# Zero fill at the head of the program, mix weights after it, convolution folding in the linear attention's steps

## The chip, the core and the metric

The kernel runs on one core of a Trainium2 chip. The metric is the device time of one execution in microseconds (us); the median of a few executions is taken. One more execution was recorded by the hardware profiler, and all times inside the kernel come from that one. The engines are named as the profile names them: PE (matrix multiplications; PEld loads their weights), DVE (vector), ACT (scalar, activations), POOL (general purpose) and SP, which only issues transfers. ACT and POOL issue transfers too. An engine works through its own list of instructions in order; an ending "q" (SPq, ACTq) marks the part that waits and issues.

## What is computed

Two layers of a graph network act on 1250 nodes with 512 channels and 40000 edges. The first layer adds three branches to the input: an attention over the edges, a linear attention over all nodes, and a feed-forward part. The second layer adds a graph convolution, a global attention and a lookup among experts. Cut to what matters here:

```python
xn = layernorm(x)
# linear attention ("mix"): all nodes
k = relu(xn @ Wk + bk) + eps;  v = xn @ Wv + bv;  q = relu(xn @ Wq + bq) + eps
h = layernorm(q @ (k.T @ v) / den @ Wo + bo + xn)
mix = layernorm(relu(h @ W1 + b1) @ W2 + b2 + h)
# edge attention ("gnn"): softmax over the edges of each source node
s[e] = q[src[e]] . k[dst[e]] / 8 + att_bias[e]
# second layer: the convolution has no function between its two matrices
conv = (A @ xn @ W_gcn + b_gcn) @ W_dense + b_dense
```

Since nothing stands between `W_gcn` and `W_dense`, the kernel multiplies them once (`W_gcn @ W_dense`, kept as `wgd_d`) and once the bias (`b_gcn @ W_dense + b_dense + b_proj`, kept as `bsum_d`). A third small product, `fold_q`, is that of the second layer's query weights with the vector `w_q`. These three are "the convolution's folding" below; nothing reads them before the second layer.

## The kernel before, in words

The edge attention is done on a dense table: `adj` in device memory has one row of nine numbers for each of 1280 x 1280 (source, target) pairs, eight for the heads' summed exp(bias) and one for the count of edges, 59 MB in all. Three things make it.

* **The fill.** Lines 221 to 228 write zeros: POOL clears a small tile `zrow`, and SP issues four transfers of 14400 KB and a small one.
* **The edge steps.** `scatter_edges` (L303) is a generator: each `pump(1)` runs one step over six columns of 128 edges, and there are 53 steps, of two batches of three columns (105 batches). A step loads keys (`kr`, L311), DVE compares them (`eq` at L325, `eqx` at L335), PE adds the weights of equal keys (L317), and DVE leaves sums and row numbers (`tot` L342, `idx` L348).
* **The scatter.** POOL issues one indirect transfer for each column, 313 in all (L351), that adds 128 rows of `tot` to `adj`. The first needs the whole fill. `tot` and `idx` have 48 buffers.

When all edges are in, SP loads `adj` in ten slabs of 5760 KB (L652), and the edge attention begins.

Between fill and slabs lies the dense work, into which the edge steps are woven by `pump` calls:

* A: normalise `xn`, transpose it (L157, L168, L171). `x` comes by the ACT queue.
* B: keys and values of the linear attention, ten tiles of 128 nodes (L487 to L493): per tile four matmuls with Wk and four with Wv, then `kp` and `va` on DVE, which add rows of `mixrows`. Wk, Wv and mixrows come by the ACT queue (L454 to L456).
* C: `kv` (L502). D: queries `qpT` (L514).
* E: ten steps, one per tile (L524 to L545): attention, Wo, layer norm, `h`.
* F: its feed-forward part, ten tiles (L556 to L566).
* G, H: weights of the edge attention, `zT`, `kT` and `q_d` (L583 to L605). I: values `gva` (L606 to L610).
* J: the convolution's folding (L613 to L635), with its own loads of 1024 KB weights, its results stored by SP.

A second generator, `weight_products` (L400), computes other products of weights (`fs` on ACT, L419) in pieces; `next(products)` runs one piece in each of the steps of C, D and E until it is used up, which in the list of PE is in the third step of E.

A transfer's end is told by one of eight semaphores (DMAHW0 to 7) that SP's and ACT's transfers take in turn. A transfer that takes a semaphore waits until the last one with the same semaphore has ended. So a transfer of one queue can wait for one of the other; such waits stand in the built instruction list next to those on data.

Of the kernel before, what the change touches and what calls it, by code (L numbers as in the profile page):

```python
# [66 lines left out]
def tile_gps_layers(ctx: ExitStack, tc: tile.TileContext, a, out):  # L67
# [12 lines left out]

    def ps_tr(shape=(P, 512), name="tr"):
        return psum.tile(list(shape), F32, tag="tr", bufs=2, name=name)


    ident = const.tile([P, P], F32, name="ident")
# [107 lines left out]
        mm(ps, [(w[:, c, m * P:(m + 1) * P], xT[:, c, c0:c0 + cn]) for c in range(xT.shape[1])])  # L193


    adj = dram.tile([NROW, CH], F32, name="adj")
    key_d = dram.tile([EC, P], F32, name="key_d")
    cnt_d = dram.tile([NP, NP], F32, name="cnt_d")
    q_d = dram.tile([P, KC, NP], F32, name="q_d")
    xm_d = dram.tile([NP, C], F32, name="xm_d")  # L200
    xb_d = dram.tile([NP, C], F32, name="xb_d")
    att_d = dram.tile([P, KC, NP], F32, name="att_d")
    deg_d = dram.tile([P, NP], F32, name="deg_d")
    w1f_d = dram.tile([NEXP, P, KC, 256], F32, name="w1f_d")
    wgd_d = dram.tile([P, KC, C], F32, name="wgd_d")
    wqd_d = dram.tile([P, KC, NKEYS], F32, name="wqd_d")
    bsum_d = dram.tile([P, C], F32, name="bsum_d")

    s_xn = ctx.enter_context(ExitStack())
    pxn = s_xn.enter_context(tc.tile_pool(name="xn", bufs=1, side="right"))
    xn = pxn.tile([P, NT, C], F32, tag="xn", name="xn")

    s_edge = ctx.enter_context(ExitStack())
    pe = s_edge.enter_context(tc.tile_pool(name="edge", bufs=1, side="right"))
    s_tmp = ctx.enter_context(ExitStack())
    ptmp = s_tmp.enter_context(tc.tile_pool(name="edgetmp", bufs=1, side="right"))

    zrow = pe.tile([P, 1800], F32, name="zrow")
    nc.gpsimd.memset(zrow, 0.0)
    adj_p = adj[0:NKEY, :].rearrange("(p r) c -> p (r c)", p=P)
    step = 16 * 1800
    for z0 in range(0, NKEY * CH // P, step):
        nc.sync.dma_start(adj_p[:, z0:z0 + step].rearrange("p (a f) -> p a f", f=1800),
                            zrow[:, None, :].to_broadcast([P, 16, 1800]))
    nc.sync.dma_start(adj[NKEY:NROW, :].rearrange("(p r) c -> p (r c)", p=P), zrow[:, :(G + 1) * CH])

    def edge_column(name, src, width, dt, fill):  # L230
        t = ptmp.tile([P, EC, width] if width > 1 else [P, EC], dt, name=name)
# [71 lines left out]
    def scatter_edges():  # L303
# [3 lines left out]
        def load_keys(c0):  # L307
            cn = min(G + B, EC - c0)
            kr = pew.tile([P, (G + B) * P], F32, name="kr")
            queue = nc.scalar if c0 == 0 else nc.sync  # L310
            queue.dma_start(kr[:, :cn * P],  # L311
                            bass.AP(tensor=key_d.tensor, offset=key_d.offset + c0 * P, ap=[[0, P], [1, cn * P]]))
            return kr
# [24 lines left out]
                add_pairs(acc, eq, n, weights(c), fresh and c == 0)  # L338

        def scatter(acc, cnt, c0, g, place):  # L340
            tot = pew.tile([P, B, CH], F32, name="tot", bufs=48)
            nc.vector.tensor_reduce(tot[:, :g], acc[:, :g].rearrange("p c (t n) -> p c n t", t=3),  # L342
                                    axis=AX.X, op=OP.add)
            row = pew.tile([P, B], F32, name="row")
            nc.vector.scalar_tensor_tensor(row[:, :g], cnt[:, :g], 1.0, keyrel[:, c0:c0 + g],
                                           op0=OP.is_equal, op1=OP.mult)
            idx = pew.tile([P, B], I32, name="idx", bufs=48)
            nc.vector.tensor_tensor(idx[:, :g], row[:, :g], spare[:, place:place + g], op=OP.add)  # L348
            near, cur = (scattered[-1] if scattered else []), []
            for c in range(g):  # L350
                st = nc.gpsimd.indirect_dma_start(  # L351
                    out=adj, out_offset=bass.IndirectOffsetOnAxis(ap=idx[:, c:c + 1], axis=0),
                    in_=tot[:, c, :], in_offset=None, compute_op=OP.add)
                for x in cur + near:
                    tc.declare_no_dep(st.ins, x.ins, reason="rows of a batch and of the one next to it differ")
                for x in (scattered[-2] if len(scattered) > 1 else []):
                    tc.add_manual_dep(st.ins, x.ins.name, SYNC, reason="rows of batches may agree")
                cur.append(st)
            scattered.append(cur)
# [40 lines left out]
    def weight_products(pool):  # L400


        def turned(name):
            wT = pool.tile([P, KC, C], F32, tag="fwT", name=name + "T")
            for k in range(KC):
                if k % 2 == 0:
                    w = pool.tile([P, KC, 256], F32, tag="fw", name="fw", bufs=2)
                    nc.sync.dma_start(w, a[name].rearrange("(c p) o -> p c o", p=P)[:, :, k * P:(k + 2) * P])
                ps = ps_tr((P, KC, P))
                for c in range(KC):  # L410
                    nc.tensor.transpose(ps[:, c, :], w[:, c, k % 2 * P:(k % 2 + 1) * P], ident)
                nc.scalar.copy(wT[:, k, :].rearrange("p (c q) -> p c q", c=KC), ps)
            return wT

        def product(wT, w, m, to):
            ps = ps_mm((P, 256))
# [25 lines left out]
                    yield  # L442

    with (tc.tile_pool(name="mix", bufs=1) as pm, tc.tile_pool(name="mixw", bufs=2) as pw,
# [3 lines left out]
        for t in range(NT):  # L451
            n = TAIL if t == NT - 1 else P
            nc.scalar.dma_start(xn[:n, t, :], a["x"][t * P:t * P + n, :])
        wk = load_w(pm, "L0_mix_Wk", KC, C, bufs=2, eng=nc.scalar)  # L454
        wv = load_w(pm, "L0_mix_Wv", KC, C, bufs=2, eng=nc.scalar)
        rows = rows_bc(pm, a["mix_rows"], len(MIX_ROWS), name="mixrows", eng=nc.scalar)  # L456

        def row(name):
            return rows[:, MIX_ROWS.index(name), :]
# [122 lines left out]
    with tc.tile_pool(name="gqkv", bufs=2) as pq:  # L582
# [23 lines left out]
        for t in range(NT):  # L606
# [1 line left out]
            node_mm(ps, zT, t, wv)  # L608
            nc.vector.tensor_tensor(va[:, t, :], ps, gbv[:, 0, :], op=OP.add)
            pump(1)  # L610


        brow = rows_bc(pq, a["l1_rows"], len(L1_ROWS), name="l1rows")  # L613
        wg = load_w(pq, "gcn_WgT", KC, C, bufs=3)
        wd = load_w(pq, "L1_gnn_W_dense", KC, C, bufs=3)
        wqn = load_w(pq, "l1_Wq", KC, C, bufs=3)
        for m in range(KC):
            ps = ps_mm()
            mm(ps, [(wg[:, c, m * P:(m + 1) * P], wd[:, c, :]) for c in range(KC)])
            qs = pq.tile([P, 512], F32, tag="qs", name="qs", bufs=3)  # L620
            nc.scalar.copy(qs, ps)
            nc.sync.dma_start(wgd_d[:, m, :], qs)
            pump(1)
        ps = ps_mm()
        mm(ps, [(col("gcn_b", c).to_broadcast([P, P]), wd[:, c, :]) for c in range(KC)])
        qs = pq.tile([P, 512], F32, tag="qs", name="qs", bufs=3)
        nc.vector.tensor_tensor(qs, ps, brow[:, 0, :], op=OP.add)
        nc.vector.tensor_tensor(qs, qs, brow[:, 1, :], op=OP.add)
        nc.sync.dma_start(bsum_d, qs)
        bd = pq.tile([P, KC, H], F32, name="bd")  # L630
        nc.vector.tensor_tensor(bd, own_head, col("l1_wq", 0, 4)[:, :, None].to_broadcast([P, KC, H]), op=OP.mult)
        ps = ps_tr((P, KC, H))
        for m in range(KC):
            mm(ps[:, m, :], [(wqn[:, c, m * P:(m + 1) * P], bd[:, c, :]) for c in range(KC)])
        nc.scalar.copy(fold_q[:, :, :H], ps)  # L635
        pump(EC)
    s_edge.close()
    s_xn.close()
# [1353 lines left out]
```

## Time and profile before

| what | us |
|---|---|
| median of three executions | 2455.51 (2454.69 to 2459.25) |
| profiled execution | 2448.96 |
| its span, first to last instruction | 2447.2 |
| PE busy | 2001.3 (82%) |
| DVE busy | 1523.3 (62%) |
| POOL busy | 696.5 (28%) |
| first and last scatter issued | 175.32, 772.57 |
| last `gva` (end of I) begins | 776.64 |
| first slab issued | 797.86 |
| first scores of the edge attention | 816.07 |

The profiled execution's time is its span and 1.8 us around it, and lies 6.6 us below the median. In the rows of the profile the first two numbers are the start and the length in us, if nothing else is said. "xN" is a number of instructions. A fp32 matmul of the program counts twice in the trace. "[0.30 <-X]" is how long the engine was idle before the instruction, and what ended that. In a table by stretches, each engine has its busy time in the stretch; after them stand the TensorE clock that was granted (1.00 is full), the busy share of the transfer engines, and the GB/s that they moved.

### The profile page before, as it was taken

The page shows a single profiled execution, that of the slowest core. Times are in us where ns is not written, and L with a number is a line of the kernel's source. Part 1 is how long each engine was busy: PE and PEld are TensorE (multiplying, and loading weights), DVE is VectorE, ACT ScalarE, POOL GpSimd, SP SyncE. Part 2 cuts the span into 40 slices and gives each one's busy share as a digit, 9 for nine tenths or more (in the row PEclk, how much of TensorE's full clock was granted, in tenths as well). Part 3 has the DMA queues.
Part 4 walks back from the last instruction along what each step waited for, and adds up shares of the span by engine and source line. Part 5 has one row for each costly group of instructions (what it writes and reads, how often), then busy time and mean ns, then how long its engine had stood idle before and what let it go on. Part 6 is the DMA issues. An engine that isn't in the chain of part 4 may idle for free.

```text
span 2447.2 us, 29595 instructions
## 1 busy us (share of the span) xinstructions
PE 2001.3 (82%) x10548; PEld 1182.2 (48%) x10548; DVE 1523.3 (62%) x4868; ACT 789.3 (32%) x1483; POOL 696.5 (28%) x448
## 2 busy tenths in 40 slices
PE   0299697684499699999799988999999999978853
PEld 0146465442245366666445445567444545555521
DVE  3539858789891599999432444456222233499998
ACT  0101001010000467777331255556211123244553
POOL 2018888888885000000000000000000000045665
PEclk9999788775699799999899999999899999989975
DMA  9987554345643666554510100000410002000000
GB/s 393 422 349 188 101 116 64 42 87 108 153 89 77 248 233 226 193 222 145 177 64 22 49 1 1 1 1 1 153 35 26 26 9 69 22 22 9 10 9 16
DMA packets 132591, 255.78 MB, mean 105 GB/s; under 512 B 51677, under 2 KB 87190, under 8 KB 130780
## 3 DMA queue, kind: packets, MB, share of 16 engines
q1 hardware_dynamic: 80576, 234.11, 25.8%
q0 software_dynamic: 46512, 8.02, 7.0%
q10 hardware_dynamic: 5356, 11.77, 1.3%
q8 instruction: 83, 1.36, 0.2%
q14 instruction: 64, 0.52, 0.1%
HBM read 161.05 MB, written 92.80 MB: 104 GB/s over the span
## 4 chain that ended last, share of the span: by engine, by line
PE 58%; DVE 23%; ACT 8%; DMA 7%; issue 2%; POOL 1%; ACTq 0%; SPq 0%; DVEq 0%; POOLq 0%
PE mm L179 32%; DVE eqx L335 4%; PE one L727 4%; PE sc L678 4%; ACT wT L718 3%; DVE eq L325 3%; PE one L717 2%; PE av L1107 2%; PE ag L1376 2%; PE one L1094 2%; PE sc L1053 2%; DMA adj<-zrow 2%; DMA mixrows<-in_mix_rows 2%; DVE sc L1736 2%; POOL adj L351 1%
## 5 line engine op out<-in xcount | busy, mean ns | idle before, releaser
L351 POOL DMA_INDIRECT adj<-tot,idx x313 | 499.9, 1597 | 260.4 <-DMA kr<-key_d 161.5
L707 DVE SCALAR_TENSOR_TENSOR ex<-ex,slab 128x1280 f32<-128x1280 f32 x80 | 197.2, 2504 | 0.0
L1307 DVE SCALAR_TENSOR_TENSOR X<-mm,gate,X 128x512 f32<-128x512 f32 x80 | 60.0, 750 | 198.6 <-PE mm L179 198.5
L335 DVE TENSOR_SCALAR_CACHE_REDUCE eqx<-kr,key 128x384 bf16<-128x384 f32 (+1 forms) x312 | 175.2, 598 | 0.1
L1245 POOL MEMSET padded<- 128x128 f32 x3 | 0.5, 204 | 580.6 <-DVE faT L1128 580.6
L325 DVE SCALAR_TENSOR_TENSOR eq<-kr,key,upto 128x128 bf16<-128x128 f32 (+2 forms) x313 | 145.8, 475 | 17.2 <-PE even L317 17.2
L717 PE MATMUL one<-ident,ex 128*128 128x128 f32 x800 | 126.3, 286 | 23.9 <-ACT wT L718 20.4
L718 ACT COPY wT<-one 128x512 f32<-128x512 f32 (+1 forms) x240 | 115.8, 516 | 90.8 <-PE one L717 86.0
L179 PE MATMUL mm<-w,hT 128*128 128x512 f32 (+1 forms) x320 | 143.6, 600 | 0.0
L179 PE MATMUL mm<-faT,w 128*128 128x512 f32 (+1 forms) x384 | 140.0, 518 | 0.7 <-ACT bs L1127 0.7
L688 DVE CUSTOM_DVE_ANT_0 ex<-sc,none 128x1280 f32<-128x1280 f32 x80 | 115.7, 1485 | 13.2 <-PE sc L678 11.9
L678 PE MATMUL sc<-kT,q 64*128 64x512 f32 (+1 forms) x480 | 104.5, 559 | 21.5 <-DMA q<-q_d 18.3
L717 PEld LDWEIGHTS one<-ident,ex 128*128 128x128 f32 x800 | 84.4, 141 | 67.5 <-ACT wT L718 48.5
L664 POOL DMA_DIRECT2D deg_d<-cnt x10 | 8.4, 844 | 357.7 <-ACT attT L734 314.5
L1096 DVE COPY wT<-one 128x512 f32<-128x512 f32 (+3 forms) x72 | 37.6, 559 | 114.9 <-PE one L1094 107.8
L700 ACT ACTIVATE ex<-ex,low 128x1280 f32<-128x1280 f32 x80 | 104.7, 1360 | 11.8 <-DVE low L693 11.7
L179 PEld LDWEIGHTS mm<-faT,w 128*128 128x128 f32 x384 | 73.9, 193 | 66.3 <-issue 65.0
L727 PE MATMUL one<-wT,gva 128*64 128x128 f32 x1600 | 100.1, 282 | 3.5 <-ACT wT L718 1.9
L317 PEld LDWEIGHTS <-eq 128*128 128x128 bf16 x625 | 43.0, 102 | 119.7 <-DVE eq L325 84.8
L1301 ACT ACTIVATE hT<-mm,cols 128x512 f32<-128x512 f32 (+1 forms) x48 | 29.0, 607 | 216.5 <-PE mm L179 216.4
L179 PEld LDWEIGHTS mm<-w,hT 128*128 128x128 f32 (+1 forms) x320 | 60.8, 190 | 75.2 <-issue 75.2
L727 PEld LDWEIGHTS one<-wT,gva 128*64 128x64 f32 x1600 | 90.5, 141 | 13.3 <-ACT wT L718 13.3
(494 smaller groups left out, 4164.6 us busy)
## 6 DMA issues: line engine op xcount, KB each, us to landing
adj<-zrow SPq DMA_DIRECT2D x4, 14400.0 KB
slab<-adj SPq DMA_DIRECT2D x10, 5760.0 KB
kr<-key_d SPq DMA_DIRECT2D x50, 576.0 KB
cnt_d<-cnt SPq DMA_DIRECT2D x10, 640.0 KB
deg_d<-cnt POOLq DMA_DIRECT2D x10, 640.0 KB, 7.4
adjT<-cnt_d SPq DMA_DIRECT2D x5, 1280.0 KB
adj<-tot,idx POOLq DMA_INDIRECT x313, 3.4
fw<-in_L_ffn_W SPq DMA_DIRECT2D x8, 512.0 KB
```

The costliest lines, as they stand in the source:

```text
L179: nc.tensor.matmul(ps, lhsT=l, rhs=r, start=i == 0, stop=i == len(pairs) - 1)
L325: nc.vector.scalar_tensor_tensor(eq[:, :n], kr[:, k0 * P:k0 * P + n], key[:, c0 + c:c0 + c + 1], upto[:, B - 1 - c:, :].rearrange("p c x - ...
L335: nc.vector.tensor_scalar(eq[:, :n * P], kr[:, k0 * P:(k0 + n) * P], key[:, c0 + c:c0 + c + 1], None, op0=OP.is_equal, op1=OP.add, accum_o ...
L351: st = nc.gpsimd.indirect_dma_start(out=adj, out_offset=bass.IndirectOffsetOnAxis(ap=idx[:, c:c + 1], axis=0), in_=tot[:, c, :], in_offset ...
L678: nc.tensor.matmul(sc[e][:, d0:d0 + dn], lhsT=q[half(e), m, :], rhs=kT[half(e), m, d0:d0 + dn], start=True, stop=True)
L688: nc.vector.tensor_tensor_reduce(out=ex, in0=sc[e][:, :NP], in1=none, scale=-0.125, scalar=-LOWEST, op0=OP.add, op1=OP.min, accum_out=low[ ...
L700: nc.scalar.activation(exs[e], exs[e], AF.Exp, bias=low[:, e:e + 1], scale=-1.0)
L707: nc.vector.scalar_tensor_tensor(exs[e], exs[e], 1.0, sl[:, :, hd], op0=OP.mult, op1=OP.mult, accum_out=den[:, hd:hd + 1])
L717: nc.tensor.transpose(ps[:, k, :], weights[t, m][e][:, (d0 + k) * P:(d0 + k + 1) * P], ident)
L718: nc.scalar.copy(wT[:, d0:d0 + dn, :], ps[:, :dn])
L727: nc.tensor.matmul(av[half(e), 0, :], lhsT=va[:, d, hd * D:(hd + 1) * D], rhs=turned[e][:, d, :], start=d == 0, stop=d == NT - 1)
L1307: nc.vector.scalar_tensor_tensor(X[:r, t, :], ps[:r], gate[:r, t, e:e + 1], X[:r, t, :], op0=OP.mult, op1=OP.add)
```

## The change

1. The fill is the first thing in the program, ahead of the constants. `zrow` is cleared by DVE instead of POOL. The five transfers are kept in a list.
2. Wk, Wv and mixrows are loaded by SP instead of ACT, and each waits until all five transfers of the fill have ended. The second load of keys goes by ACT as the first does; from the third on they go by SP.
3. `tot` and `idx` have 32 buffers instead of 48.
4. The folding leaves part J. It becomes the end of `weight_products`, in halves of 256 columns instead of 512, and so runs in the later steps of E.

```diff
+    zrow = pe.tile([P, 1800], F32, name="zrow")
+    nc.vector.memset(zrow, 0.0)
...
+    fill = [nc.sync.dma_start(adj_p[:, z0:z0 + step].rearrange("p (a f) -> p a f", f=1800),
+                              zrow[:, None, :].to_broadcast([P, 16, 1800]))
+            for z0 in range(0, NKEY * CH // P, step)]
+    fill.append(nc.sync.dma_start(adj[NKEY:NROW, :].rearrange("(p r) c -> p (r c)", p=P), zrow[:, :(G + 1) * CH]))
...
     ident = const.tile([P, P], F32, name="ident")
...
-    zrow = pe.tile([P, 1800], F32, name="zrow")
-    nc.gpsimd.memset(zrow, 0.0)
...
-            queue = nc.scalar if c0 == 0 else nc.sync
+            queue = nc.scalar if c0 < 2 * G else nc.sync
...
-            tot = pew.tile([P, B, CH], F32, name="tot", bufs=48)
+            tot = pew.tile([P, B, CH], F32, name="tot", bufs=32)
...
-            idx = pew.tile([P, B], I32, name="idx", bufs=48)
+            idx = pew.tile([P, B], I32, name="idx", bufs=32)
...
+        def fetched(name):
+            return load_w(pool, name, KC, C, tag="fwT")
+
+        def half_of(name, x):
+            w = pool.tile([P, KC, 256], F32, tag="fw", name="fw", bufs=2)
+            nc.sync.dma_start(w, a[name].rearrange("(c p) o -> p c o", p=P)[:, :, x * 256:(x + 1) * 256])
+            return w
...
+        wT = fetched("gcn_WgT")
+        for x in range(2):
+            o = slice(x * 256, (x + 1) * 256)
+            w = half_of("L1_gnn_W_dense", x)
+            for m in range(KC):
+                product(wT, w, m, wgd_d[:, m, o])
+                if m % 2:
+                    yield
...
+            ps = ps_mm((P, 256))
+            mm(ps, [(col("gcn_b", c).to_broadcast([P, P]), w[:, c, :]) for c in range(KC)])
+            f = pool.tile([P, 256], F32, tag="fs", name="fs", bufs=2)
+            nc.vector.tensor_tensor(f, ps, fb[:, 0, :], op=OP.add)
+            nc.vector.tensor_tensor(f, f, fb[:, 1, :], op=OP.add)
+            nc.sync.dma_start(bsum_d[:, o], f)
+        wT = fetched("l1_Wq")
...
+            mm(ps[:, m, :], [(wT[:, c, m * P:(m + 1) * P], bd[:, c, :]) for c in range(KC)])
+        nc.scalar.copy(fold_q[:, :, :H], ps)
...
-        wk = load_w(pm, "L0_mix_Wk", KC, C, bufs=2, eng=nc.scalar)
-        wv = load_w(pm, "L0_mix_Wv", KC, C, bufs=2, eng=nc.scalar)
-        rows = rows_bc(pm, a["mix_rows"], len(MIX_ROWS), name="mixrows", eng=nc.scalar)
+        late = [nc.sync.dma_start(wk, a["L0_mix_Wk"].rearrange("(c p) o -> p c o", p=P)),
+                nc.sync.dma_start(wv, a["L0_mix_Wv"].rearrange("(c p) o -> p c o", p=P)),
+                nc.sync.dma_start(rows, bass.AP(tensor=a["mix_rows"].tensor, offset=a["mix_rows"].offset,
+                                                ap=[[0, P], [C, len(MIX_ROWS)], [1, C]]))]
+        for ld in late:
+            for x in fill:
+                tc.add_manual_dep(ld.ins, x.ins.name, SYNC, reason="the zeros go first")
...
-        brow = rows_bc(pq, a["l1_rows"], len(L1_ROWS), name="l1rows")
-        wg = load_w(pq, "gcn_WgT", KC, C, bufs=3)
-        wd = load_w(pq, "L1_gnn_W_dense", KC, C, bufs=3)
-        wqn = load_w(pq, "l1_Wq", KC, C, bufs=3)
-        for m in range(KC):
-            ps = ps_mm()
-            mm(ps, [(wg[:, c, m * P:(m + 1) * P], wd[:, c, :]) for c in range(KC)])
...
-            nc.sync.dma_start(wgd_d[:, m, :], qs)
-            pump(1)
...
-        nc.scalar.copy(fold_q[:, :, :H], ps)
         pump(EC)
```

In the built lists of instructions, these are the places where the two kernels part. ACT's list begins with the loads of constants and edges, then nine tiles of `x`; the fifth tile of `x` takes the semaphore of the fill's first transfer and waits for its end, and the fill's second transfer takes the semaphore of the eighth tile of `x` and waits for that. On DVE, batches 0 to 4 stand ahead of the first use of mixrows, the tiles of B stand among batches 5 to 21, where before all of B stood ahead of batch 2; from batch 30 on the order of dense work and edges is that of before, with the folding's pieces in steps 4 to 9 of E. SP's list has kr, Wk, Wv, mixrows, kr, kr behind the fill. From the first slab on, all five lists are those of before.

## The prediction

> **What bounds the kernel now.** I read the chain of waits first: up to the first scores (816.07 us) it changes engine all the time, so I went stage by stage through the table by stretches and the order of time of single engines. First the start (stretches, then pieces of the chain):
>
> ```profile
> 0.00:10.00 10.00, 0.00 (x0) 0.00 (x0) 4.30 (x8) 0.00 (x0) 9.10 (x22) 1.00 0.79 271
> 40.00:50.00 10.00, 0.00 (x0) 0.00 (x0) 0.00 (x0) 0.00 (x0) 0.00 (x0) 1.00 1.02 425
> 160.00:170.00 10.00, 10.00 (x25) 4.50 (x24) 2.50 (x4) 0.00 (x0) 0.00 (x0) 1.00 1.02 417
> 170.00:180.00 10.00, 10.00 (x24) 4.38 (x24) 2.92 (x5) 0.00 (x0) 4.07 (x3) 1.00 0.52 149
> ```
>
> ```profile
> 11.11 43.09 DMA adj<-zrow
> 54.28 0.50 ACTq L269
> 59.73 41.42 DMA mixrows<-in_mix_rows
> ```
>
> The transfer engines are full (about 419 GB/s) from 10 to some 173 us. The second fence shows a semaphore in common: ACT's key store waits until the fill's first transfer ends at 54.2.
>
> The scatter and the end of this part, as POOL, PE and SP have them:
>
> ```profile
> 175.32 1.78 POOL L351 DMA_INDIRECT adj<-tot,idx  x1 [161.50 <-DMA kr<-key_d]
> 177.40 1.57 POOL L351 DMA_INDIRECT adj<-tot,idx  x1 [0.30 <-issue]
> ...
> 772.57 1.54 POOL L351 DMA_INDIRECT adj<-tot,idx  x1 [0.30 <-issue]
> ```
>
> ```profile
> 776.44 13.90 PE L179 MATMUL mm<-L_gnn_W_dense,gcn_WgT 128*128 128x512 f32 x32
> 790.18 3.60 PE L179 MATMUL mm<-L_gnn_W_dense,cols 128*128 128x512 f32 x8
> 793.61 4.18 PE L179 MATMUL tr<-bd,l_Wq 128*128 128x8 f32 x32
> 816.07 4.55 PE L678 MATMUL sc<-kT,q 64*128 64x512 f32 x12 [18.29 <-DMA q<-q_d]
> ```
>
> POOL issues 313 scatters almost without a pause, 597.3 us from first to last. It is done at 774.1 (landed at 777.5, with the median 3.4 us), while SP issues the first slab only at 797.86, when the folding (21.7 us of PE) ends. So two chains end near 777, fill + scatter and the dense work up to `gva` (DVE, 776.64 + 0.69), and the folding lies behind both.
>
> **Folding out of the end.** From the end of `gva`, 777.3, to the slab's issue at 797.86 are 20.5 us, all on the path. They go whole, if nothing else is late. Then the slab comes at the later of the two chains. From the slab on all lists are those of before, so its shift is the whole change.
>
> **Fill.** Fill bytes: 59.0 MB. By the stretches about 70.2 MB have moved when the fill ends: the 170:180 row holds 1.49 MB, 3.6 us of a full row, so it ends at some 173.5. In the changed order Wk, Wv and mixrows (4.2 MB) and two tiles of x and a row (0.8) come after it and a second kr (0.6) before: 65.8 MB. `zrow` on DVE: a memset of 512 columns takes 0.48, so 1800 take 1.7, and the fill is issued at about 2.6, not 11.1; the first ten us then hold 3.3 MB. End: 10 + 62.5 / 0.419 = 159. The new waits on semaphores take some back. ACT's fifth x waits for the fill's first transfer; the second waits for ACT's eighth x. First transfer: 14.7 MB beside 3.7 MB of loads, about 1 of these before it starts: ends near 47. Then four issues of 1 us (the two at 54.82 took 2.10), 2.5 us to land, 2.5 us until the next zeros flow: the fill stands still for 9 us, in which x moves 1.3 MB (3 us of work). Cost 6: **fill ends at 165.5**. Bounds: 160 (the wait is hidden) and 172 (a second stop). I take the row's own numbers.
>
> Here a rule speaks against the change. The Trainium skill, "DMA: Bandwidth & Descriptors", Specifications, gives device memory 358 GB/s per core. By it 65.8 MB end at 190 and the slab at 794, a gain of 4. The rows above show 417 to 425 for 160 us of just these bytes: I keep 165.5.
>
> **Scatter.** First one 1.8 us behind the fill, as before: 167.3. Rows for it are ready: batches 0 to 4 need only the two kr of ACT and one just behind the fill, and DVE idles before. Last landed: 167.3 + 602.2 = **769.5**. 32 buffers cost nothing: counted in the trace, DVE is at most 11 batches ahead of POOL.
>
> **Waiting weights.** Wk is issued at 166, behind it Wv, mixrows (4.2 MB) and the kr in front of it (0.6): at 0.37 to 0.42 MB/us mixrows is there at 180; Wk at 171. Before, the first matmul with Wk ran at 105.22. So B starts some 65 us later; queued behind it in PE's order are all of C to I, on SP the keys from the fourth step on. What takes it in:
>
> ```profile
> 200.00:220.00 20.00, 19.64 (x170) 16.37 (x170) 17.44 (x84) 3.67 (x10) 16.46 (x11) 0.83 0.85 200
> 220.00:240.00 20.00, 19.25 (x145) 11.46 (x144) 19.60 (x97) 1.49 (x4) 16.95 (x11) 1.00 0.67 144
> 240.00:260.00 20.00, 12.02 (x109) 6.69 (x107) 19.99 (x102) 0.37 (x1) 16.65 (x12) 0.76 0.52 99
> 260.00:280.00 20.00, 8.89 (x90) 5.19 (x90) 19.97 (x96) 0.00 (x0) 16.65 (x12) 0.50 0.49 92
> 700.00:725.00 25.00, 24.00 (x142) 11.09 (x140) 24.91 (x116) 2.06 (x3) 21.04 (x14) 1.00 0.53 103
> ```
>
> Before, B ran 105 to 181 with keys locked out behind the fill, and then DVE did batches 2 to 29 alone, 188 to 280, 6.5 us a step, PE half idle. Now both run together. The last row is such a place: eight matmuls and one edge step in 7.15 us (eqx at 684.50, 691.65, 698.79), PE and DVE both full. A tile of B with its step: DVE 6.5 + 0.69 + 0.41 + 0.69 = 8.3, PE 16 x 0.43 + edges = 7.2 to 8; DVE decides. Two tiles without edges until 187, eight at 8.3: 253 (batch 21); four steps to batch 29 at 6.5: 279, and 3 for keys queued behind Wq and Wo: **282**, against 279.1 before. PE then has 42 products and 20 matmuls of D to the mark of batch 34 (42 x 0.47 + 20 x 0.86 + edges = 39): 321, against 324.7. So the delay is gone: -3. If B and edges took turns (6.9 more for each of eight tiles) it would be +52.
>
> The skill's same page, Rules for kernel authors, says "Issue the DMA early, do compute, wait on its semaphore late". That is against holding the weights back, and by it B's 65 us would be lost: 777.3 + 65, 44 behind the old slab, 2499. The rows say that DVE, not PE, is behind at 280; I take them.
>
> **Folding inside E.** PE gets 16.0 + 1.8 x 2 + 4.2 us of it in steps 4 to 9. Steps with and without products now:
>
> ```profile
> 386.00:399.00 13.00, 10.63 (x73) 7.42 (x73) 12.25 (x53) 2.12 (x5) 11.13 (x7) 1.00 0.51 90
> 428.00:443.00 15.00, 9.99 (x60) 6.37 (x60) 12.61 (x58) 1.37 (x3) 12.56 (x9) 0.73 0.33 42
> ```
>
> The first is a step with eight products, the second one without. The one with more work is shorter, since PE's clock is 1.00 and not 0.73 (Wo's eight take 3.54 at one, 6.44 at the other). Five steps get such a load: 5 x -2.3 = -11. Bounds: -12, and +22 if each us of PE is added to the chain. I take -11, from the nearest rows. The folding's DVE pieces (4 x 0.45) and stores are lost in waits of 2 to 4 us a step.
>
> F is DVE at 10.65 a tile, H and I as they are. `gva` ends at 777.3 - 3 - 11 = **763**; the scatter at 769.5 is last. Slab at 771: gain 27 less a us for a wait that ends later. Sum: -26 us, 2423 for the profiled execution's 2448.96. The median of the runs lies 6.6 above that; from it, 2455.5 - 26 = **2429**.
>
> **Rivals.**
>
> * *The folding is paid where it goes.* For: E is a chain with PE in it, and 22 us are added. Against: the two rows above. `gva` 777.3 - 3 + 22 = 796, slab 797: 2454, no change.
> * *B and the edges take turns* (slower). In-order lists with three PSUM banks and three `eq` buffers: PE waits for compared keys, DVE for PE. Price up to 55 us on B; `gva` at 763 + 55 = 818, slab 20 late: 2476. It decides from a delay of 34 us on B. Against it: the row at 700.
> * *The dense chain is last, not the scatter:* part of E's or B's gain doesn't come, `gva` at 775 to 790: 2435 to 2448.
> * *The fill never stops:* it ends at 160, and the dense chain at 763 decides: 2422.
>
> **How the numbers follow.** Forecast (2425 to 2434) 0.48; dense chain last 0.19; no stop 0.05; these are faster by over 0.2%, which is about what a measurement of this kernel can tell from no change: 0.72. Paid where it goes: 0.12, same. Taking turns 0.16, slower. Range 2419 to 2458: from below the best case to the end of "same"; only the slower rival is left out.
>
> **What would show it.** Transfers near idle for some us at about 50; first scatter at 167, last issued at 765; first Wk matmul at 169 to 171; batch 29 near 282; E's steps 4 to 8 near 13 us at a clock near 1; slab at 771 right behind the last scatter. Wrong if the fill stops twice, if DVE waits for PE in B (busy under 90% between 190 and 280), or if E's steps grow.

## The result, and the profile after

| | kernel before | changed kernel |
|---|---|---|
| median, runs alternating on the same chip | 2455.24 (20 runs) | 2460.54 (20 runs) |
| span of the profiled execution | 2447.2 | 2458.3 |
| first and last scatter issued | 175.32, 772.57 | 168.53, 788.83 |
| last `gva` ends | 777.3 | 804.7 |
| first slab issued | 797.86 | 804.77 |

The changed kernel takes 1.0022 times as long, with a 95% interval of 1.0012 to 1.0032: slightly slower, where 2429 us (a ratio of 0.989) was forecast. The profiled execution of the kernel before lies 6.3 us below its median, that of the changed kernel (2460.32 us) at its median. So the two profiles are 11 us apart where the medians are 5.3 apart, and a few us of any difference between them belong to the single executions.

Everything below numbers the batches of the edge steps from 0 and gives a batch the time at which DVE begins its `tot`. Line numbers are those of the kernel that is shown; in the changed kernel L209 is `mm`, L326 and L336 the comparisons, L352 the scatter, L670 the slab.

The same stretches as before, in the changed kernel (columns: stretch, its length, then busy us and number of instructions of PE, PEld, DVE, ACT and POOL, then TensorE's clock, busy share of the transfer engines, GB/s):

```profile
40.00:50.00 10.00, 0.00 (x0) 0.00 (x0) 0.00 (x0) 0.00 (x0) 0.00 (x0) 1.00 0.78 314
160.00:170.00 10.00, 0.57 (x6) 0.37 (x6) 1.49 (x7) 0.00 (x0) 1.47 (x1) 0.50 0.79 292
200.00:220.00 20.00, 19.12 (x111) 9.24 (x110) 19.73 (x86) 0.00 (x0) 16.76 (x11) 1.00 0.48 83
260.00:280.00 20.00, 19.54 (x184) 15.90 (x183) 20.00 (x100) 3.39 (x10) 16.95 (x11) 1.00 0.77 183
280.00:300.00 20.00, 19.99 (x117) 15.44 (x116) 10.08 (x47) 2.79 (x8) 15.80 (x11) 0.83 0.59 115
300.00:320.00 20.00, 20.00 (x70) 13.11 (x69) 2.25 (x3) 2.23 (x6) 16.65 (x12) 1.00 0.54 88
```

The first row is the fill's stop, and the second its end. The four others are what matters. Before, PE had 8.89 us of work in 260:280 while DVE was full. Now PE is full in each of the four, and from 280 on DVE has 10 and then 2 us of work in 20: PE has become the bound.

The scatter on POOL, and the end of the stage on PE and SP (first two numbers: start and length):

```profile
168.53 1.78 POOL L352 DMA_INDIRECT adj<-tot,idx  x1 [156.43 <-issue]
...
788.83 1.54 POOL L352 DMA_INDIRECT adj<-tot,idx  x1 [0.30 <-issue]
```

```profile
769.47 34.50 PE L209 MATMUL mm<-gnn_WvT,zT 128*128 128x512 f32 x80
822.52 3.79 PE L696 MATMUL sc<-kT,q 64*128 64x512 f32 x8 [18.55 <-DMA q<-q_d]
```

```profile
804.77 0.32 SPq L670 DMA_DIRECT2D slab<-adj  x1
```

The folding is gone: `gva`'s matmuls are the last thing on PE, and the slab follows 0.1 us behind the last `gva`. But `gva` itself ends 27.4 us later than before. At the slab that makes +27.4 - 20.5 = +6.9 us. The scatter starts 7 us earlier and ends 16 us later, because batches now reach POOL too late, near batch 60 and batch 90; it still ends 11 us ahead of the slab and decides nothing. From the slab to the end it is 1653.5 us, before 1649.3; in the fifteen profiles of this study, whose lists are the same from there on, it lies between 1649.3 and 1656.6, so these 4 us are within the spread of single executions.

Where the 27 us arise is told by four marks:

| mark | before | after | difference |
|---|---|---|---|
| batch 29 | 279.1 | 289.2 | +10.1 |
| batch 30 | 293.6 | 321.4 | +27.8 |
| first `at` of E | 358.4 | 386.2 | +27.8 |
| last `gva` ends | 777.3 | 804.7 | +27.4 |

It is all there by batch 30, and nothing is added or given back behind it. Between batch 29 and batch 30 stand the first four groups of D, whose results DVE takes from PE as `qpT`. In the kernel before, three of the four are ready when DVE comes to them:

```profile
279.29 0.73 DVE L514 TENSOR_SCALAR qpT<-mm,bqe 128x512 f32<-128x512 f32 x1
280.07 0.74 DVE L514 TENSOR_SCALAR qpT<-mm,bqe 128x512 f32<-128x512 f32 x1
280.80 0.74 DVE L514 TENSOR_SCALAR qpT<-mm,bqe 128x512 f32<-128x512 f32 x1
289.45 0.75 DVE L514 TENSOR_SCALAR qpT<-mm,bqe 128x512 f32<-128x512 f32 x1 [4.69 <-PE mm L179]
```

In the changed kernel DVE waits for PE before each of them:

```profile
296.53 0.75 DVE L557 TENSOR_SCALAR qpT<-mm,bqe 128x512 f32<-128x512 f32 x1 [3.74 <-PE mm L209]
303.41 0.75 DVE L557 TENSOR_SCALAR qpT<-mm,bqe 128x512 f32<-128x512 f32 x1 [6.13 <-PE mm L209]
310.30 0.75 DVE L557 TENSOR_SCALAR qpT<-mm,bqe 128x512 f32<-128x512 f32 x1 [6.14 <-PE mm L209]
317.19 0.75 DVE L557 TENSOR_SCALAR qpT<-mm,bqe 128x512 f32<-128x512 f32 x1 [6.14 <-PE mm L209]
```

### The profile page after: what moved, and what is told of

The parts are those of the page before. It is cut to its first block, busy times and chain, and to the rows that moved or that the text cites. A ratio compares the mean times of both kernels' runs of the same rounds, so it can differ in the third digit from the quotient of the medians.

```text
span 2458.3 us, 29737 instructions
## 1 busy us (share of the span) xinstructions
PE 1995.2 (81%) x10588; PEld 1190.1 (48%) x10588; DVE 1529.1 (62%) x4875; ACT 788.4 (32%) x1484; POOL 695.9 (28%) x447
## 4 chain that ended last, share of the span: by engine, by line
PE 56%; DVE 20%; ACT 8%; DMA 2%; issue 2%; POOL 1%; DVEq 0%; ACTq 0%; SPq 0%; POOLq 0%
PE mm L209 30%; PE one L745 4%; PE sc L696 4%; ACT wT L736 3%; DVE eqx L336 3%; PE one L735 2%; PE av L1125 2%; PE ag L1394 2%; DVE eq L326 2%; PE one L1112 2%; PE sc L1071 2%; DVE sc L1754 2%; DVE ix L1695 1%; DVE ix L1704 1%; DVE rest L1707 1%
## 5 line engine op out<-in xcount | busy, mean ns | idle before, releaser
L352 POOL DMA_INDIRECT adj<-tot,idx x313 | 501.0, 1601 | 277.2 <-issue 228.0
L326 DVE SCALAR_TENSOR_TENSOR eq<-kr,key,upto 128x128 bf16<-128x128 f32 (+2 forms) x313 | 145.9, 478 | 85.7 <-DMA kr<-key_d 68.9
L336 DVE TENSOR_SCALAR_CACHE_REDUCE eqx<-kr,key 128x384 bf16<-128x384 f32 (+1 forms) x312 | 176.1, 600 | 0.0
L209 PE MATMUL mm<-w,hT 128*128 128x512 f32 (+1 forms) x320 | 145.4, 606 | 0.0
L209 PE MATMUL mm<-faT,w 128*128 128x512 f32 (+1 forms) x384 | 140.2, 518 | 0.7 <-ACT bs L1145 0.7
L706 DVE CUSTOM_DVE_ANT_0 ex<-sc,none 128x1280 f32<-128x1280 f32 x80 | 115.8, 1485 | 15.6 <-PE sc L696 14.5
L209 PEld LDWEIGHTS mm<-faT,w 128*128 128x128 f32 x384 | 73.3, 191 | 67.2 <-issue 66.1
L209 PEld LDWEIGHTS mm<-w,hT 128*128 128x128 f32 (+1 forms) x320 | 61.5, 193 | 76.4 <-issue 76.4
```

What stands on the lines that cost most here:

```text
L209: nc.tensor.matmul(ps, lhsT=l, rhs=r, start=i == 0, stop=i == len(pairs) - 1)
L326: nc.vector.scalar_tensor_tensor(eq[:, :n], kr[:, k0 * P:k0 * P + n], key[:, c0 + c:c0 + c + 1], upto[:, B - 1 - c:, :].rearrange("p c x - ...
L336: nc.vector.tensor_scalar(eq[:, :n * P], kr[:, k0 * P:(k0 + n) * P], key[:, c0 + c:c0 + c + 1], None, op0=OP.is_equal, op1=OP.add, accum_o ...
L352: st = nc.gpsimd.indirect_dma_start(out=adj, out_offset=bass.IndirectOffsetOnAxis(ap=idx[:, c:c + 1], axis=0), in_=tot[:, c, :], in_offset ...
L706: nc.vector.tensor_tensor_reduce(out=ex, in0=sc[e][:, :NP], in1=none, scale=-0.125, scalar=-LOWEST, op0=OP.add, op1=OP.min, accum_out=low[ ...
```

## The experiments

The theory to test: the wait of Wk, Wv and mixrows costs some 27 us of the dense chain, the moved folding gives its 20 us, and the early fill gives nothing. Rivals: the folding costs in E what it saves in J, or the early fill itself does the harm.

### Each part alone

**fold_only**: the kernel before, with the end of `weight_products` from the changed kernel and without part J.

> The kernel before with one part of the change alone: the folding leaves the end of the convolution's stage and goes into the weight products; the fill, the loads of Wk, Wv and mixrows, and the 48 tot buffers stay. Theory (the wait put on Wk, Wv and mixrows holds the linear attention up by 27 us, and the moved folding gives its 20.5 us): gva ends near 777 us as before, the slab's transfer is issued at 777 to 781 instead of 797.9, and the time is 2455 - 20 = 2435 us. Rival (the moved products cost in stage E what they save at the end): the mark of the tenth ln output comes some 20 us after 502, the slab is issued at about 797, and the time is 2455 us.

**wait_only**: the changed kernel, with part J of the kernel before put back.

> The changed kernel with the folding put back at the end of the convolution's stage; the fill first, the wait of Wk, Wv and mixrows and the 32 tot buffers stay. Theory: the dense chain is 27 us late and the folding is on its end again: gva ends at 804, the slab is issued at about 825, and the time is 2455 + 27 = 2482 us. Rival (the moved products in stage E are what makes E and the slab late): without them E is as short as before, the slab is issued at about 800 and the time is 2455 to 2460 us.

**no_wait**:

```diff
-        late = [nc.sync.dma_start(wk, a["L0_mix_Wk"].rearrange("(c p) o -> p c o", p=P)),
...
-        for ld in late:
-            for x in fill:
-                tc.add_manual_dep(ld.ins, x.ins.name, SYNC, reason="the zeros go first")
+        wk = load_w(pm, "L0_mix_Wk", KC, C, bufs=2, eng=nc.scalar)
+        wv = load_w(pm, "L0_mix_Wv", KC, C, bufs=2, eng=nc.scalar)
+        rows = rows_bc(pm, a["mix_rows"], len(MIX_ROWS), name="mixrows", eng=nc.scalar)
```

> The changed kernel, but Wk, Wv and mixrows are loaded by ACT behind x, as in the kernel before, and wait for nothing; the fill first, the moved folding and the 32 tot buffers stay. Theory: the k/v tiles run while the fill does, batch 34 is reached at about 325 us, gva ends near 777 and the slab is issued at 777 to 783; 2435 us, as with the folding alone. Rival (the early fill itself is the cost: its stop, its sharing with x, the third keys' load behind it, or the fewer buffers): batch 34 stays near 352, the slab near 804 and the time near 2460 us.

**fill_first**: the edit of no_wait, and part J put back.

> The kernel before with the fill issued first of all and 32 tot buffers; the weights do not wait and the folding stays at the end of the convolution's stage. Theory: the first scatter goes some 7 us earlier, at 168, but the end of stage J (gva, then the folding) sets the slab, so it stays near 798 us and the time at 2455 us, within 4 us. Rival (the early fill itself costs the dense chain): slab at 820 or later, 2475 us or more.

| kernel | median | ratio, 95% interval | batch 34 | last `gva` ends | slab |
|---|---|---|---|---|---|
| fold_only | 2433.1 | 0.9908, 0.9896 to 0.9921 | 326.1 | 778.6 | 778.7 |
| wait_only | 2482.0 | 1.0108, 1.0093 to 1.0122 | 351.3 | 806.5 | 827.1 |
| no_wait | 2431.2 | 0.9906, 0.9892 to 0.9921 | 321.6 | 774.4 | 777.3 |
| fill_first | 2447.5 | 0.9976, 0.9966 to 0.9986 | 322.5 | 775.0 | 795.2 |

The kernel before had 2455.3 us in these runs, and batch 34 at 324.7 in its profile. On the wait and the folding the theory holds in all four. The wait costs 2482.0 - 2447.5 = 34 us with the folding in J, and 2460.5 - 2431.2 = 29 with the folding in E. The moved folding gives 22 us in fold_only, 21 with the wait (2482.0 to 2460.5) and 16 in no_wait (2447.5 to 2431.2), where the last scatter comes to set the slab. So the folding is not paid where it goes, and the wait is all of the loss.

fill_first is some 8 us faster than the kernel before, more than I allowed. Its slab comes 2.7 us earlier (its first `va` comes at 103.5 instead of 121.0). The profiled executions are only 2.0 us apart (2446.92 and 2448.96), since that of the kernel before lies so far below its median; the other 6 us have no place in these two profiles. I had its first scatter wrong too: it goes at 179.2, not 168, and at 179.8 in no_wait, later than the 175.3 of the kernel before. With the folding moved, the early fill makes 2 us (2433.1 to 2431.2), which is not to be told from nothing.

### Whose time is it that the wait costs?

The work up to batch 34 in four stretches, first in no_wait (columns as above):

```profile
90.00:165.00 75.00, 74.73 (x250) 35.62 (x247) 35.68 (x135) 5.11 (x14) 0.00 (x0) 1.00 1.01 418
165.00:183.00 18.00, 7.23 (x66) 6.27 (x65) 3.21 (x15) 2.98 (x8) 2.87 (x2) 0.81 1.01 363
183.00:276.00 93.00, 74.69 (x570) 52.18 (x570) 82.10 (x402) 7.09 (x19) 78.07 (x50) 0.76 0.68 148
276.00:322.00 46.00, 45.02 (x216) 30.48 (x217) 23.47 (x96) 4.47 (x12) 38.56 (x25) 0.94 0.56 108
```

and the changed kernel:

```profile
90.00:165.00 75.00, 10.85 (x80) 8.56 (x80) 14.26 (x78) 5.45 (x12) 0.00 (x0) 0.62 1.01 417
165.00:183.00 18.00, 11.68 (x33) 5.20 (x34) 7.22 (x32) 0.00 (x0) 9.50 (x6) 0.61 0.93 333
183.00:289.00 106.00, 103.46 (x677) 61.13 (x675) 95.68 (x412) 5.48 (x17) 87.75 (x56) 0.98 0.61 125
289.00:352.50 63.50, 63.02 (x294) 41.82 (x292) 23.36 (x96) 6.70 (x18) 53.13 (x35) 0.98 0.55 100
```

Each group of rows ends at batch 34. Read PE's column as length less busy time, which is its idle time. In no_wait PE stands idle for 0.3 + 10.8 + 18.3 + 1.0 = 30.4 us. In the changed kernel it is 64.2 + 6.3 + 2.5 + 0.5 = 73.5: nearly all of it under the fill, and 9 us behind it. That is 43 us more idle time. Against it stands 12.7 us less busy time (189.0 against 201.7); from the start to batch 34 both kernels have 1119 instructions on PE. The clock fits: 0.98 in the last two rows, against 0.76 and 0.94 in no_wait. 43.1 - 12.7 = 30.4, and batch 34 comes 352.5 - 321.6 = 30.9 later. DVE's column has gaps too: 61 us in the first row, most of it with no keys, but also 50 us in the last two, so DVE isn't full when the time is lost.

That is an account and no test: DVE's idle time, read in the same way, is 34 us more as well (122.0 against 87.5). Four runs meant as a test told something else, and a fifth decides. (Their expectations call C and D together stage C.)

**wait_quarter** and **no_wait_quarter**: both leave out three quarters of the multiplications of every product of weights.

```diff
-            mm(ps, [(wT[:, c, m * P:(m + 1) * P], w[:, c, :]) for c in range(KC)])
+            mm(ps, [(wT[:, c, m * P:(m + 1) * P], w[:, c, :]) for c in range(1)])
```

> The changed kernel with the weight products (w_q with peer_down, Wo with the expert weights, gcn_WgT with the dense weights) made of one of their four partial products each: three quarters of their multiplications are left out, while every load, copy and store of them stays. To be read against the same cut in the kernel without the wait. Theory (the wait costs because TensorE is then without a gap from 180 to 320 us, and the products of stage C have no cover): the stretch from batch 29 to batch 30 falls from 32 us to 16 to 20, and batch 34 comes within 10 to 15 us of the same cut without the wait, where the whole products leave 30. Rival (VectorE's 52 us without keys are what is lost, whatever TensorE has to do): batch 34 stays 25 to 30 us behind the cut kernel without the wait.

> The kernel without the wait (fill first, folding moved, Wk, Wv and mixrows by ACT behind x) with the same cut: three quarters of the weight products' multiplications are left out. Theory: the products of stages B and C lie beneath VectorE's work here, so batch 34 comes at 315 to 322, at most 6 us before the 321.6 of the whole products, and the time falls only by what stage E gives, to 2422 to 2431 us, with the last scatter setting the slab. Rival (TensorE bounds stage C here too): batch 34 comes 10 us or more earlier.

Measured: 2434.7 us (0.9926, 0.9913 to 0.9939) and 2429.6 us (0.9909, 0.9893 to 0.9925). With the wait, the stretch from batch 29 to batch 30 falls from 32.2 to 12.5 us. But batch 34 comes at 327.0 and 296.7: both kernels won 25 us, and the gap stays at 30. For batch 34 the rival's numbers came out in both runs. But the two rivals don't go together: the second has PE as the bound without the wait too. The products of stage D have no cover in either kernel (PE 45.02 of 46 us in the last row of no_wait), so to cut them shortens both alike and says nothing of the gap. The whole time of no_wait_quarter lies in the expected range for another reason: the last scatter, issued at 773.5, sets the slab at 776.7, though `gva` ends at 751.4. And with fewer products E did not get shorter: in wait_quarter it took 176.5 us instead of 164.8 from the first `at` to F.

**products_early**: the products moved under the fill, to give PE work where it stands idle.

```diff
+        for _ in range(13):
+            next(products, None)
```

with the products' loads and stores on ACT instead of SP.

> The changed kernel, all three weights still waiting, but 13 steps of the weight products (w_q turned, its four products with peer_down, Wo turned, some twenty products with the expert weights) stand ahead of the k/v tiles, and their loads and stores go through ACT's queue, so that they can run at 110 to 165 us, where TensorE stood still. Theory (what is lost is TensorE's time under the fill; the products have no cover left in stages C and D): the stretch from batch 29 to batch 30 falls from 32 us to 15 or 20, batch 34 comes at 325 to 337 instead of 352, gva ends at 777 to 790, and the time is 2435 to 2447 us. Rival (what is lost is VectorE's time: 52 us with no keys under the fill, which the k/v tiles no longer fill): batch 34 stays near 350 and the time at 2455 to 2462 us.

Measured: 2529.6 us (1.0307, 1.0293 to 1.0321). The waits of SP's queue show what happened (columns: what waits, for what, us in all, times, longest):

```profile
SPq L109 <- DMA w1f_d<-fs: 134.5, 2, 89.6
SPq L109 <- DMA key_d<-kt: 52.4, 1, 52.4
```

L109 is the fill. Its later transfers took the semaphores of ACT's stores of products and waited 134.5 us for them. The fill moved 206 GB/s at 110 to 165 us, and the first scatter went at 235.3. The run answers nothing about PE; it shows what the common semaphores can do.

**products_pool**: as products_early, but with seven steps, and their loads and stores on GpSimd's queue.

> The changed kernel, the three weights waiting, with seven steps of the weight products ahead of the k/v tiles (w_q turned, four products with peer_down, Wo turned, eight products with expert weights), this time with their loads and stores on GpSimd's queue, which is idle until the first scatter, so that neither ACT nor the fill's own issues stand behind them. It is some 37 us of TensorE's work (12 products at 1.73, two weights turned at about 5, the gate's small products at 6), and 5 MB of transfers, 12 us of the fill's rate. Theory (what the wait costs is TensorE's time under the fill: from the first k/v tile to batch 34 it has 166 us of work and no gap): TensorE is busy some 35 us more before the first k/v tile and as much less behind it; from the first va to batch 34 it takes 130 to 140 us instead of 169, batch 34 comes at 325 to 335, and the time is 2430 to 2445 us. Rival (VectorE's time without keys is what is lost): from the first va to batch 34 it stays 160 to 170 us, batch 34 comes at 352 to 365, and the time is 2460 to 2473 us.

Measured: 2490.0 us (1.0133, 1.0116 to 1.0150). The fill kept its rate, the first `va` came at 195.8 and batch 34 at 360.4, 164.6 us later. That looks like the rival, but the kernel isn't the one that the expectation describes: stages C and D pull sixteen pieces of the generator whatever was taken before, so the seven were missing from E and not from D. E shows it: from the first `at` to F it took 180.3 us instead of 164.8.

**products_pool_c** mends that:

```diff
-                next(products, None)
+                if (c0 // 512) * KC + m >= 7:
+                    next(products, None)
```

> As the kernel with seven steps of the weight products ahead of the k/v tiles on GpSimd's queue, and the one thing that run had wrong mended: stage C took the same sixteen steps as ever, so that the seven were missing from stage E and not from C. Here the first seven of the twelve pulls in stage C are left out, so that C has seven steps (14 products, 24 us of TensorE) less and E its seven again. Theory (what the wait costs is TensorE's time under the fill): from the first va to batch 34 it takes 140 to 148 us instead of 164.6 there and 169 in the changed kernel; batch 34 comes at 336 to 344, E takes 165 us again instead of 180, and the time is 2442 to 2454 us, with the fill still 12 us late. Rival (VectorE's time without keys is what is lost): from the first va to batch 34 it stays 160 us or more, and the time is 2466 us or more.

Measured: 2448.7 us (0.9977, 0.9963 to 0.9991), as the theory has it and faster than the kernel before, with the wait in place and the fill 13 us later. Its stretches:

```profile
90.00:165.00 75.00, 44.88 (x226) 37.59 (x223) 16.59 (x89) 11.41 (x27) 8.19 (x13) 0.80 1.01 416
196.00:300.00 104.00, 101.17 (x659) 58.44 (x658) 96.35 (x415) 4.28 (x15) 86.07 (x55) 1.00 0.55 115
300.00:337.00 37.00, 36.53 (x169) 19.12 (x169) 23.13 (x95) 1.12 (x3) 30.90 (x21) 1.00 0.45 77
```

PE now has 34 us more of work under the fill (44.88 against 10.85) and 3.3 us of gaps in the 141 behind it. From the first `va` to batch 34 it takes 139.8 us instead of 169.3. Batch 34 comes at 336.4, 16 us earlier, although the tiles of B start 13 us later. DVE still stands idle under the fill (16.59 us of work in the first row, in the changed kernel 14.26). So what the wait costs is TensorE's time under the fill. The same move was not tried without the wait; there PE has 0.3 us free from 90 to 165 us, so the pieces would find no room.

### The long step of stage E

In the changed kernel eight of the nine intervals from one `h` to the next are 12 to 16 us long, and one is 20.3.

**lwq_later**:

```diff
         wT = fetched("l1_Wq")
+        yield
```

> The changed kernel with one more stop in the weight products, between the load of l1_Wq and the small products that need it, so that these fall a step later. Theory (the step of 20.3 us in stage E is TensorE standing in front of that load, and it gives back the 6.5 us that the steps before it won): no step of E is over 16 us, gva ends at 797 instead of 804, and the time is 2460 - 6.5 = 2454 us. Rival (the step is long by its work): the long step moves by one, and the time stays at 2460 us.

Measured: 2458.2 us (1.0012, 1.0003 to 1.0022), not to be told from the changed kernel. The long interval moved to the next place (23.0 us), so the load isn't the cause, and the step is long by its work, as the rival has it. PE in lwq_later:

```profile
515.75 6.83 PE L209 MATMUL tr<-bd,l_Wq 128*128 128x8 f32 x32
```

and in the changed kernel:

```profile
495.81 6.16 PE L209 MATMUL tr<-bd,l_Wq 128*128 128x8 f32 x32
```

These are matmuls of only 8 columns, but 32 passes of them hold PE for 6.2 to 6.8 us. In part J of the kernel before the same passes took 4.18 us. The granted clock goes with it: 0.85 in J, 0.56 in the changed kernel and 0.50 in lwq_later, and time multiplied by clock is 3.6, 3.4 and 3.4 us. So these products grew by 2 us because they now run at a lower clock; in the changed kernel PE had stood idle for 2.39 and 0.91 us just ahead of them.

**no_wait_lwq**: no_wait with the same line.

> The kernel without the wait (fill first, folding moved, Wk, Wv and mixrows by ACT behind x), with the small products of l1_Wq one step later as well. Theory (without the wait gva and the last scatter end at the same time, so that shortening one of them brings nothing): gva at 768 instead of 774, the last scatter still issued at 772 to 775, the slab at 775 to 778, and the time at 2431 us, within 3 us. Rival (the dense chain alone is the bound): slab at 771, 2425 us.

Measured: 2430.4 us (0.9895, 0.9881 to 0.9909), `gva` at 774.5, last scatter 774.5, slab 777.6. The time is as expected, but not for the reason given: `gva` didn't come earlier. Whether a shorter dense chain alone would help is therefore not tested here.

### A better version

In no_wait the scatter is last, and it starts at 179.8, 11 us later than in the changed kernel: 4.2 MB of weights go during the fill, which is 10 us at 418 GB/s.

**weights_first**: no_wait_lwq with Wk, Wv and mixrows issued by SP ahead of the fill.

> As the kernel without the wait and with l1_Wq's products a step later, but Wk, Wv and mixrows are issued by SP ahead of the fill. Theory: the k/v tiles start at 85 to 92 instead of 102 and are over by 155, the fill ends 7 us later than in the changed kernel, so that the first scatter goes at 172 to 176 instead of 179.8 and the last at about 770; the scatter sets the slab at 772 to 775, and the time is 2428 us. Rival (the bytes cost the same wherever they stand: first scatter at 179 to 180, and the k/v tiles wait for x in any case): 2431 us.

Measured: 2426.7 us (0.9894, 0.9879 to 0.9910). First scatter 174.2, last 769.4, slab 772.5, as the theory has it; batch 34 at 311.2 and `gva` at 763.9. The k/v tiles start far earlier than I had thought, the first `va` at 52.3 (85 to 92) and the last at 133.6.

**two_rows_first** (edit against weights_first):

```diff
-                                    ap=[[0, P], [C, len(MIX_ROWS)], [1, C]]))
+    nc.sync.dma_start(two, bass.AP(tensor=a["mix_rows"].tensor, offset=a["mix_rows"].offset,
+                                   ap=[[0, P], [C, 2], [1, C]]))
...
     fill.append(nc.sync.dma_start(adj[NKEY:NROW, :].rearrange("(p r) c -> p (r c)", p=P), zrow[:, :(G + 1) * CH]))
+    nc.sync.dma_start(six, bass.AP(tensor=a["mix_rows"].tensor, offset=a["mix_rows"].offset + 2 * C,
+                                   ap=[[0, P], [C, len(MIX_ROWS) - 2], [1, C]]))
```

> As the kernel with Wk, Wv and mixrows ahead of the fill, but of mixrows' eight rows only mix_bk and mix_bv go ahead of it, and the other six (1.5 MB) behind it. Theory (the scatter sets the slab, and the scatter starts when the fill's bytes are through): the fill ends 3.6 us earlier (1.5 MB at 420 GB/s), the first scatter goes at 170.5 instead of 174.2, the last at 766, the slab at 769 instead of 772.5, and the time is 2423 us. Rival (the keys' transfer behind the fill waits for the six rows too): the first scatter stays at 174, and the time at 2427 us.

Measured: **2421.3 us** (0.9869, 0.9854 to 0.9884), 32 us below the kernel before in the same runs (2453.5). Its scatter:

```profile
167.80 1.78 POOL L363 DMA_INDIRECT adj<-tot,idx  x1 [155.69 <-DMA mixsix<-in_mix_rows]
...
762.67 1.54 POOL L363 DMA_INDIRECT adj<-tot,idx  x1 [0.30 <-issue]
```

It starts 6.4 us earlier than in weights_first and not the 3.7 expected, and ends as much earlier. The 1.5 MB are 3.6 of it; for the rest, the transfer engines moved 421 GB/s from 20 to 100 us instead of 406, which is worth 2.9 us. `gva` ends at 762.7 and the slab goes at 765.7. Scatter and dense chain end together now.

## Why the prediction was wrong, point by point

`gva` ends at 804.7 and not at 763, and that sets the slab. Of these 42 us, 31 come from the waiting weights and 11 from stage E.

* **Folding out of the end.** Right: 20.5 us were expected, and fold_only gives 22.2 (slab 19.2 us earlier).
* **Fill.** Right. The stop is there at 40 to 60 us (314 and 339 GB/s instead of 418, and none at 48 to 49), Wk, which waits for the fill, is issued at 167.55 (166), and the first scatter goes at 168.53 (167.3). In my sum for the stop, the 2.5 us to land and the 2.5 us until the next zeros had no row behind them. The 358 GB/s per core of the Trainium skill ("DMA: Bandwidth & Descriptors", Specifications) did not bind here: the changed kernel's row from 90 to 165 us has 417.
* **Scatter.** The first was right, the last was not: 788.83 instead of 765, since DVE falls behind POOL with the late dense chain. It isn't on the path. That 32 buffers cost nothing fits (no_wait has them and loses nothing).
* **Waiting weights: this step failed.** First matmul with Wk at 173.0 (171), a tile of B in 8.4 us (8.3). Two terms were too small.
  - "**282**, against 279.1 before": measured 289.2. I had DVE decide, and let PE follow in 7.2 to 8 us a tile. PE was as full as DVE (19.12 of 20 us), and when DVE was to go on alone, PE still had `kv`, the products with peer_down and the gate's products to do.
  - "PE then has 42 products and 20 matmuls of D to the mark of batch 34": from batch 29 to batch 34 it has 138 passes of products (69 matmuls) and 67 of Wq (33), 32.0 + 28.3 us in place of 39 with everything. My count is near what the kernel before has left at that mark (96 passes and 43), and even there the stretch takes 45.6 us and not 39. It left out what the change pushes behind the mark. In the kernel before, PE did 48 passes of products and 24 of Wq from the end of B to batch 29, 27.2 us of its time, under DVE's edge steps. After the change that place is taken by B (7 and none), so they run with DVE idle: batch 29 to batch 30 takes 32.2 us instead of 14.5.

  Batch 34 thus came at 352.5 instead of 321: 7 us by the first term, 24 by the second, of which 18 are the displaced work. "So the delay is gone: -3" is the sentence that was wrong. I had seen that PE was half idle at 240 to 280 and gave that room to B, without counting what stood there already and had to go elsewhere.
* **The rule that I set aside.** "Issue the DMA early, do compute, wait on its semaphore late" (the Trainium skill, "DMA: Bandwidth & Descriptors", Rules for kernel authors) is right here in its direction. It names no price, only that the fixed setup cost overlaps; that all 65 us would be lost was my own reading of it. Measured: 29 to 34. The rest of the delay was taken in behind the fill, where PE has less idle time (9.3 us against 30.1 in no_wait) and a higher clock.
* **Folding inside E.** Half right. The steps with the folding's large products are shorter, as the rows of before promised: the four intervals from the fourth to the eighth `h` by 6.5 us in all. The last 4.2 us of the folding, the small products of l_Wq, I took for filling like the rest; at a clock of 0.56 they stand in the way for 6.2 us, and the last two intervals are 5.4 us longer. E took 164.8 us, before 165.0, instead of 11 less; fold_only, without the wait, has the same 164.8. The two rows that I took 2.3 us a step from are 2.0 apart, so the sum should have been 10.
* **Rivals.** "Paid where it goes" is out by fold_only. "B and the edges take turns" had the right sign, and a size that is too large (2476 for 2460.5), but not the way: in B both engines were full side by side. The sign that I had named for it did not show (DVE was busy for 86.96 of the 90 us from 190 to 280); that the kernel came out slower, as it has it, is luck. "The dense chain is last" is what happened, beyond the end it was given (804.7 for 775 to 790).

The range's upper end, 2458, was missed by 2.5 us, since it left out the one rival that put a price on the wait.

## What to carry to other kernels

An idle engine in a stage is room only once: before work is moved into it, list what the in-order list of that engine already puts there later, and give that work a new place too. A wait that looks absorbed has to be followed to the first stretch where the other engine falls idle; here DVE's 2.25 us of 20 at 300 to 320 was the sign. Where a load stands in the way of an urgent transfer, send ahead only the part that is needed first: here two rows of eight.

## What the runs showed of the hardware

* **PE's clock and the length of steps.** With no products in it but the last small ones, in its first step (products_pool), E took 180.3 us instead of 164.8, with less work. One of its other steps, columns as above:

```profile
462.00:478.00 16.00, 10.92 (x55) 6.42 (x54) 11.00 (x48) 1.37 (x3) 9.43 (x6) 0.68 0.28 40
```

  At a granted clock of 0.68 the step takes 16 us; the changed kernel's step at 463 to 476, with eight products more, takes 13 at a clock of 1.00. The Trainium skill ("TensorE: Matmul & The Clock Gate", Part 1) says that the clock follows how busy PE has been of late. The runs agree: over all of E the clock is 0.87 in the changed kernel and 0.77 in wait_quarter, which took 176.5 us with fewer multiplications. The kernel before, with three pieces of products in E, took 165.0 us at 0.81. In these runs filler work on PE goes with a stage that is up to 15 us shorter.
* **Semaphores shared by two queues.** ACT's stores, 128 KB each, held the fill back by 134.5 us in products_early, since its transfers wait for the earlier user of their semaphore, whichever queue that is. On GpSimd's queue (products_pool, with seven of the thirteen steps) they did not: the fill kept 413 to 418 GB/s from 90 to 165 us.
* **Narrow matmuls.** 32 passes of 8 columns took 6.83 us in lwq_later, 0.21 each. Just ahead of them, 4 passes of 128 columns took 1.09 us, 0.27 each. So a sixteenth of the columns saves a fifth of the time. PEld is busy all the while (6.85 of 6.85 us), so the weight loads are the likely bound; no run varied them alone.
